# One load queue in order of need, and a batch's first projections in the tail of the batch ahead

## The chip, the cores and the metric

The kernel runs on one core of one Trainium2 chip. The metric is the device time of the kernel in microseconds; a lower number is better. The engines of a core run side by side, each through its own instructions in a fixed order: TensorE (PE) multiplies matrices into PSUM, VectorE (DVE) and ScalarE (ACT) work element by element and can read PSUM, GpSimd (POOL) does so on SBUF alone, and SyncE (SP) issues DMAs. ACT can issue DMAs too.

## The reference, cut to what matters

There are 16 batches of 512 positions, each of width 512. One block of attention and one gated FFN run on each batch:

```python
x = x + layernorm(attn(layernorm(x)))       # 16 heads of 32, causal, distance bias
x = x + layernorm(ffn(layernorm(x)))

# attn(h)
q = h @ Wq_down.T @ Wq_up.T                 # rank 384
c = h @ Wkv_down.T                          # rank 128
k, v = c @ k_up, c @ v_up                   # per head
s = q k^T / sqrt(32) - slope[h] * |i - j|   # causal
out = softmax(s) @ v  @ Wo.T

# ffn(h): weights are packed 4-bit values with a scale for each group of 128
y = (silu(h @ Wg.T) * (h @ Wu.T)) @ Wd.T    # 512 -> 2 x 1408 -> 512
y / rms(y)
```

## The kernel before, in words

**Stages of a batch.** A batch is four tiles of 128 positions. `normed(b, t)` normalises one loaded tile `xl` (statistics on VectorE, the reciprocal root on GpSimd, the scaling on VectorE), transposes it on PE and lets ScalarE copy it into `xnT`. `attention_steps(b)` then makes c (`pc`), the first k and q (`pk`, `pq`), and works through 16 units: four groups of four heads, and in each group four blocks of 128 queries, so that the scores of a unit are 128, 256, 384 or 512 wide. A unit's `scores` are four matmuls, four VectorE reductions that add the distance bias and take the row maximum (L338), four exps on ScalarE (L351), a reciprocal, and four scalings on GpSimd (L357). Two units later `turn` transposes the weights (`pt`) and copies them to `pT` (three by ScalarE, one by VectorE); three units later `attend` multiplies them with v (`po`). The first four units each make one block of v too (`pv`), and the third and fourth unit of a group make the next group's q and k. `tail(t)` multiplies by Wo (`pw`, L429), normalises, adds the input, normalises again; the result is transposed (`ptf`) and split into three bf16 parts, `x2`.

**The FFN.** `ffn_steps(b)` has 11 blocks `i`. Each block makes four gate steps (`pg`) and four up steps (`pu`) of three bf16 matmuls, each evacuated by ScalarE or VectorE in turn; then four output tiles (`py`) take 11 down steps each, which need no evacuation until the tile is done. That makes 132 steps. A finished `py` tile is normalised into `z` through two reciprocal roots on GpSimd.

**What sets the order.** PE's order is written out by hand: `interleave(main, side, share)` runs the attention of batch b as the main line, and each `yield n` in it lets n FFN steps of batch b - 1 follow. Batch 0 has no FFN ahead of it; 22 steps that unpack the FFN weights (`unpack_steps`, with a load `dq` or `dqd`, two VectorE passes, and a third on ScalarE or VectorE) run beside it at a share of 0.16. After the last attention, the last FFN runs alone. On the other engines and on SyncE's queue a scheduler sets the order when the kernel is built.

**Buffers.** `ps_m` is a PSUM pool of three slots for `pc`, `pk`, `pq`, `pv`, `pw`, `pg`, `pu`, `py` and the join of the q weights (`pjq`); `ps_s` has four for scores and transposes. `xl` has two buffers. ACT's queue issues the weight loads, SyncE's all others.

The main line's yields, in its order:

```python
project c; yield 1; project k(0); yield 1; project q(0); yield 1
for n in units (+3):
    scores(n); yield 1
    if n < 4: project_v(n)
    yield 1
    q or k of the next group; yield 1
    if n >= 12: normed(b + 1, n - 12); yield 1
    attend(n - 3); yield 1
    turn(n - 2); yield 2
for t in range(5): tail(t); yield 4; transpose and split(t - 1); yield 4
```

Of the kernel before, what the change touches and what calls it, by code (L numbers as in the profile page):

```python
# [9 lines left out]
F32 = mybir.dt.float32  # L10
F16 = mybir.dt.float16
# [3 lines left out]
ALU = mybir.AluOpType  # L15
PSUM = bass.MemoryType.PSUM

P = 128
HEADS = 16
HD = 32  # L20
# [11 lines left out]
def attn_ffn_kernel(  # L32
# [46 lines left out]

    def load_w(src, rows, cols, name, pool=const, tag=None):  # L80
        w = pool.tile([P, rows // P, cols], F32, tag=tag or name, name=name)
        nc.scalar.dma_start(w, src.rearrange("(c p) n -> p c n", p=P))
        return w

    xl_tiles = {}

    def load_norm(b):
        for t in range(NT):  # L90
            xl = work.tile([P, D], F32, tag="xl", name=f"xl_{b}_{t}", bufs=2)
            nc.sync.dma_start(xl, x_in[b, t * P : (t + 1) * P, :])
            xl_tiles[b, t] = xl

    load_norm(0)
    w_kv = load_w(wkv_t, D, RKV, "w_kv")

    w_qd = load_w(wqd, RQ, D, "w_qd", work, "v")
    w_qu = load_w(wqu_t, RQ, D, "w_qu", work, "atT")
    w_vup = load_w(vup, RKV, D, "w_vup")  # L100
    w_kup = load_w(kup, RKV, D, "w_kup")
    w_o = load_w(wo_t, D, D, "w_o")
    w_q = const.tile([P, ND, D], F32, tag="w_q", name="w_q")


    w_gu = tc.dram_tile([NI, P, NGU * P], BF16, name="w_gu")
# [6 lines left out]
    nc.gpsimd.memset(mhalf, -0.5)  # L113

    dist = const.tile([P, L], F32, tag="dist", name="dist")
    nc.gpsimd.iota(
        dist, pattern=[[1, L]], base=P - L, channel_multiplier=-1,  # L120
        allow_small_or_imprecise_dtypes=True,
    )
    nc.gpsimd.affine_select(
        out=dist, in_=dist, pattern=[[-1, L]], compare_op=ALU.is_ge,
        fill=MASKED, base=L - P, channel_multiplier=1,
    )

    qscale = const.tile([P, NG], F32, tag="qscale", name="qscale")  # L130
    for g in range(NG):
        for j in range(HPG):
            nc.gpsimd.memset(
                qscale[j * HD : (j + 1) * HD, g : g + 1], SCALE / SLOPES[g * HPG + j]
            )


    shl = const.tile([P, 1], I32, tag="shl", name="shl")
    shl0 = const.tile([P, 1], I32, tag="shl0", name="shl0")
    nc.gpsimd.iota(shl0, pattern=[[0, 1]], base=0, channel_multiplier=1)  # L140
    nc.vector.tensor_scalar(shl, shl0, 7, 7, ALU.bitwise_and, ALU.bitwise_xor)
    nc.vector.tensor_scalar(shl, shl, 2, None, ALU.logical_shift_left)

    raw = work.tile([P, NI * NGU], F16, tag="raw", name="raw")
    nc.scalar.dma_start(raw, gus)
    s_gu = const.tile([P, NI * NGU], F32, tag="s_gu", name="s_gu")
    nc.gpsimd.tensor_scalar(s_gu, raw, 1.0, None, ALU.mult)
    ups = s_gu.rearrange("p (i c) -> p i c", c=NGU)[:, :, ND:]  # L150
    nc.gpsimd.tensor_scalar(ups, ups, 0.5, None, ALU.mult)

# [97 lines left out]
            pt[:, :D].rearrange("p (c n) -> p c n", n=P),  # L252
        )

    def attention_steps(b):
        xn_t = xn_ts.pop(b)

        def project(dst, lhs, rhs, n, copy, name):
            pm = ps_m.tile([P, 512], F32, tag="pm", name=name)
            for c in range(n):  # L260
                nc.tensor.matmul(pm, lhs(c), rhs(c), start=c == 0, stop=c == n - 1)  # L261
            copy(dst, pm)  # L262

        q_ts = {}

        def project_q(g):
            q_ts[g] = work.tile([P, L], F32, tag="qT", name=f"qT_{b}_{g}", bufs=2)
            project(
                q_ts[g],
                lambda c: w_q[:, c, g * P : (g + 1) * P],  # L270
                lambda c: xn_t[:, c, :],
                ND,
                lambda o, i: nc.vector.tensor_scalar(
                    o, i, qscale[:, g : g + 1], None, ALU.mult
                ),
                f"pq_{b}_{g}",
            )

        k_ts = {}

        def project_k(g):
            k_ts[g] = work.tile([P, L], F32, tag="kT", name=f"kT_{b}_{g}", bufs=2)
            project(
                k_ts[g],
                lambda c: w_kup[:, 0, g * P : (g + 1) * P],
                lambda c: c_t,
                1,
                nc.scalar.copy,
                f"pk_{b}_{g}",
            )  # L290

        c_t = work.tile([P, L], F32, tag="cT", name=f"cT_{b}")
        project(
            c_t, lambda c: w_kv[:, c, :], lambda c: xn_t[:, c, :], ND, nc.scalar.copy,
            f"pc_{b}",
        )
        yield 1
        project_k(0)
        yield 1
        if b == 0:  # L300
            join_q()
        project_q(0)
        yield 1
        v = work.tile([P, NT, D], F32, tag="v", name=f"v_{b}")

        def project_v(t):
            project(
                v[:, t, :],
                lambda c: c_t[:, t * P : (t + 1) * P],
                lambda c: w_vup[:, 0, :],  # L310
                1,
                nc.scalar.copy if t % 2 == 0 else nc.vector.tensor_copy,
                f"pv_{b}_{t}",
            )

        at_t = work.tile([P, NG, L], F32, tag="atT", name=f"atT_{b}")

        def scores(g, qb):
            w = (qb + 1) * P
            mx = small.tile([P, HPG], F32, tag="mx", name=f"mx_{b}_{g}_{qb}")  # L320
            sums = small.tile([P, HPG], F32, tag="sums", name=f"sums_{b}_{g}_{qb}")
            ps, s = [], []
            for j in range(HPG):
                rows = slice(j * HD, (j + 1) * HD)
                st = ps_s.tile([P, 512], F32, tag="s", name=f"s_{b}_{g}_{qb}_{j}")
                nc.tensor.matmul(  # L326
                    st[:, :w],
                    q_ts[g][rows, qb * P : (qb + 1) * P],
                    k_ts[g][rows, :w],
                    start=True,  # L330
                    stop=True,
                )
                s.append(st)
            for j in range(HPG):
                p = work.tile(
                    [P, w], F32, tag=f"p{qb}", name=f"p_{b}_{g}_{qb}_{j}", bufs=HPG
                )
                nc.vector.tensor_tensor_reduce(  # L338
                    p,
                    s[j][:, :w],  # L340
                    dist[:, L - w :],
                    SLOPES[g * HPG + j],
                    -3.4e38,
                    ALU.add,
                    ALU.max,
                    mx[:, j : j + 1],
                )
                ps.append(p)
            nc.vector.tensor_scalar(mx, mx, -1.0, None, ALU.mult)  # L349
            for j in range(HPG):  # L350
                nc.scalar.activation(  # L351
                    ps[j], ps[j], AF.Exp, bias=mx[:, j : j + 1],
                    accum_out=sums[:, j : j + 1],
                )
            nc.vector.reciprocal(sums, sums)  # L355
            for j in range(HPG):
                nc.gpsimd.tensor_scalar(  # L357
                    ps[j], ps[j], sums[:, j : j + 1], 1.0, ALU.mult, ALU.mult
                )
            return ps  # L360
# [36 lines left out]
        for n in range(len(units) + lag2):  # L397
            if n < len(units):
                g, qb = units[n]
                made[n] = scores(g, qb)  # L400
                yield 1
                if n < NT:
                    project_v(n)
                yield 1
                if g + 1 < NG and qb == 2:
                    project_q(g + 1)
                elif g + 1 < NG and qb == 3:
                    project_k(g + 1)
                yield 1
                if b + 1 < B and n >= len(units) - NT:  # L410

                    normed(b + 1, n - (len(units) - NT))
                    yield 1
                if n == len(units) - NT:
                    load_x(b)
            if 0 <= n - lag2 < len(units):
                attend(*units[n - lag2], turned.pop(n - lag2))
                yield 1
            if 0 <= n - lag < len(units):
                turned[n - lag] = turn(*units[n - lag], made.pop(n - lag))  # L420
                yield 2
# [19 lines left out]
            return y  # L441

        ys = {}
        for t in range(NT + 1):
            if t < NT:
                ys[t] = tail(t)
                yield 4
            if t > 0:
                y = ys.pop(t - 1)
                pt = transpose_block(  # L450
# [90 lines left out]

    for t in range(NT):
        normed(0, t)
    for b in range(B):
        if b + 1 < B:
            load_norm(b + 1)
        if b == 0:
            interleave(attention_steps(b), unpack_steps(), 0.16)
        else:
            interleave(attention_steps(b), ffn_steps(b - 1))  # L550
# [52 lines left out]
```

## Time and profile before

| what | us |
|---|---|
| median of 3 runs | 3367.75 (3363.11 to 3371.17) |
| the profiled execution | 3367.57, span 3365.8 |
| PE busy | 3027.8 (90% of the span) |
| VectorE busy | 1894.0 (56%) |
| GpSimd busy | 1712.2 (51%) |
| ScalarE busy | 1557.2 (46%) |
| first scores of batch 0 on PE | at 51.79 |
| first Wo matmul of batch 0 | at 174.09 |
| first c matmul of batch 1 | at 209.01 |
| first gate matmul of the last FFN | at 3251.87 |

The span runs from the first to the last instruction of one profiled execution; the time of that execution stands beside it. In a line of a timeline the columns are the start, the length, the engine, the source line, the operation with the tile written and the tiles read, the shapes, and how many instructions were merged; the bracket is the engine's idle time just before, and what ended it.

### The profile page before, as it was taken

What the parts mean: (1) busy time and instruction counts of PE and PEld (TensorE: products, weight loads), DVE (VectorE), ACT (ScalarE), POOL (GpSimd) and SP (SyncE); (2) the same over time, 40 slices, a digit from 0 to 9 for tenths busy, and PEclk for the clock granted to TensorE, in tenths of its full rate; (3) what the DMA queues carried; (4) which work ended last, traced back from release to release, by engine and by line L of the source; (5) the groups of instructions that cost most, each with busy time, mean ns of one, the idle gap of its engine ahead of it and who ended that gap; (6) DMA issues with size and microseconds to landing.
All of it is one profiled execution on the core that took longest, in us unless ns stands there. A gap on an engine that the chain in (4) does not pass through costs nothing.

```text
span 3365.8 us, 49620 instructions
## 1 busy us (share of the span) xinstructions
PE 3027.8 (90%) x17304; PEld 1500.1 (45%) x17304; DVE 1894.0 (56%) x4937; ACT 1557.2 (46%) x4016; POOL 1712.2 (51%) x2412
## 2 busy tenths in 40 slices
PE   5879999989998899999999999899989999999998
PEld 2434444444444444444444444444444444444443
DVE  3556465564655556465564655646465564655643
ACT  3536264462635526264362634626255362644622
POOL 2245454554545546454554545545455554545554
PEclk9889999999999999999999999999999999999999
DMA  5201001111010100101011010101101010001000
GB/s 158 85 26 32 30 28 32 32 32 32 23 35 29 33 32 26 35 26 35 29 32 32 23 35 29 35 29 29 35 23 38 26 33 29 29 26 32 23 26 25
DMA packets 61866, 116.07 MB, mean 34 GB/s; under 512 B 6832, under 2 KB 8752, under 8 KB 61616
## 3 DMA queue, kind: packets, MB, share of 16 engines
q1 hardware_dynamic: 59328, 109.47, 10.6%
q10 hardware_dynamic: 2288, 3.43, 0.3%
q8 instruction: 137, 2.24, 0.3%
q14 instruction: 113, 0.93, 0.1%
HBM read 93.21 MB, written 19.66 MB: 34 GB/s over the span
## 4 chain that ended last, share of the span: by engine, by line
PE 46%; DVE 21%; POOL 15%; ACT 11%; issue 4%; DMA 2%; POOLq 0%; SPq 0%; ACTq 0%; DVEq 0%
PE py L507 10%; DVE p L338 8%; PE pg L481 7%; ACT p L351 7%; PE pq L261 7%; PE pu L481 6%; PE pt L371 5%; PE pw L429 4%; PE po L384 3%; PE s L326 3%; POOL p L357 3%; POOL g L497 3%; POOL hT L503 2%; POOL u L497 1%; ACT u L491 1%
## 5 line engine op out<-in xcount | busy, mean ns | idle before, releaser
L357 POOL TENSOR_SCALAR p<-p,sums 128x128 f32<-128x128 f32 (+3 forms) x1024 | 550.5, 556 | 426.2 <-DVE sums L355 291.3
L351 ACT ACTIVATE p<-p,mx 128x128 f32<-128x128 f32 (+3 forms) x1024 | 561.6, 550 | 416.5 <-DVE mx L349 416.4
L481 PEld LDWEIGHTS <-wi 128*128 128x128 bf16 x4224 | 385.6, 98 | 756.3 <-issue 452.9
L507 PE MATMUL py<-w_dn,hT 128*128 128x512 f32 x1408 | 656.1, 598 | 0.0
L481 PE MATMUL pg<-x,wi 128*128 128x512 bf16 x2112 | 541.3, 380 | 117.4 <-ACT kT L262 32.7
L481 PE MATMUL pu<-x,wi 128*128 128x512 bf16 x2112 | 533.9, 382 | 67.7 <-DVE g L493 49.4
L338 DVE CUSTOM_DVE_ANT_0 p<-s,dist 128x128 f32<-128x128 f32 (+3 forms) x1024 | 443.7, 485 | 51.2 <-PE s L326 49.1
L497 POOL TENSOR_TENSOR u<-u,u 128x512 f32<-128x512 f32 x176 | 229.0, 1301 | 349.7 <-DVE u L493 347.6
L371 PE MATMUL pt<-ident,p 128*128 128x128 f32 x2560 | 339.3, 278 | 34.2 <-ACT xnT L250 27.9
L507 PEld LDWEIGHTS py<-w_dn,hT 128*128 128x128 f32 x1408 | 252.1, 190 | 261.6 <-issue 255.6
L497 POOL TENSOR_TENSOR g<-g,g 128x512 f32<-128x512 f32 x176 | 223.4, 1269 | 273.3 <-DVE g L493 273.3
L373 ACT COPY pT<-pt 128x128 f32<-128x128 f32 (+3 forms) x768 | 273.7, 427 | 175.0 <-PE pt L371 116.4
L371 PEld LDWEIGHTS pt<-ident,p 128*128 128x128 f32 x2560 | 301.1, 143 | 111.0 <-POOL p L357 38.3
L491 ACT ACTIVATE g<-pg,s_gu 128x512 f32<-128x512 f32 x352 | 242.2, 688 | 224.3 <-PE pg L481 223.3
L493 DVE SCALAR_TENSOR_TENSOR u<-pu,s_gu,u 128x512 f32<-128x512 f32 x352 | 263.3, 748 | 114.0 <-ACT u L491 105.8
L493 DVE SCALAR_TENSOR_TENSOR g<-pg,s_gu,g 128x512 f32<-128x512 f32 x352 | 263.5, 749 | 82.8 <-ACT g L491 52.6
L491 ACT ACTIVATE u<-pu,s_gu 128x512 f32<-128x512 f32 x352 | 239.4, 680 | 76.1 <-PE pu L481 76.1
L326 PE MATMUL s<-kT,qT 32*128 32x128 f32 (+3 forms) x2048 | 246.5, 489 | 24.4 <-DVE pT L373 7.6
L355 DVE RECIPROCAL sums<-sums 128x4 f32<-128x4 f32 x256 | 45.5, 178 | 388.6 <-ACT p L351 388.6
L261 PE MATMUL pq<-xnT,w_q 128*128 128x512 f32 x512 | 243.5, 620 | 17.1 <-DVE g L493 17.1
L231 ACT CAST x<-ptf 128x512 bf16<-128x512 f32 x64 | 37.3, 583 | 473.2 <-PE ptf L225 473.2
L429 PE MATMUL pw<-w_o,atT 128*128 128x512 f32 x512 | 232.0, 596 | 0.0
(82 smaller groups left out, 3305.7 us busy)
## 6 DMA issues: line engine op xcount, KB each, us to landing
wi<-w_gu SPq DMA_DIRECT2D x176, 256.0 KB, 2.6
xl<-x_in SPq DMA_DIRECT2D x64, 256.0 KB, 2.6
x<-x_in SPq DMA_DIRECT2D x64, 256.0 KB, 2.6
out<-x SPq DMA_DIRECT2D x64, 256.0 KB, 2.0
dq<-gup SPq DMA_DIRECT2D x11, 512.0 KB, 4.8
w_gu<-wq SPq DMA_DIRECT2D x11, 256.0 KB, 2.0
dqd<-dnp SPq DMA_DIRECT2D x11, 256.0 KB, 3.8
sc<-dns SPq DMA_DIRECT2D x11, 128.0 KB, 3.4
```

Of the source, the lines that this page charges most:

```text
L261: nc.tensor.matmul(pm, lhs(c), rhs(c), start=c == 0, stop=c == n - 1)
L326: nc.tensor.matmul(st[:, :w], q_ts[g][rows, qb * P : (qb + 1) * P], k_ts[g][rows, :w], start=True, stop=True,)
L338: nc.vector.tensor_tensor_reduce(p, s[j][:, :w], dist[:, L - w :], SLOPES[g * HPG + j], -3.4e38, ALU.add, ALU.max, mx[:, j : j + 1],)
L351: nc.scalar.activation(ps[j], ps[j], AF.Exp, bias=mx[:, j : j + 1], accum_out=sums[:, j : j + 1],)
L357: nc.gpsimd.tensor_scalar(ps[j], ps[j], sums[:, j : j + 1], 1.0, ALU.mult, ALU.mult)
L371: nc.tensor.transpose(pt[:, cols], ps[j][:, cols], ident)
L429: nc.tensor.matmul(pm[:, :D], at_t[:, g, t * P : (t + 1) * P], w_o[:, g, :], start=g == 0, stop=g == NG - 1,)
L481: nc.tensor.matmul(pm[:, :L], wi[:, o, :], x2_p[b][:, n, c, :], start=n == 0, stop=n == 2,)
L491: nc.scalar.activation(to, pm[:, :L], AF.Copy, scale=s)
L493: nc.vector.scalar_tensor_tensor(to, pm[:, :L], s, to, ALU.mult, ALU.add)
L497: nc.gpsimd.tensor_tensor(acc, acc, add, ALU.add)
L507: nc.tensor.matmul(pm[:, :D], h_t[:, i, t * P : (t + 1) * P], w_dn[:, i, :], start=i == 0, stop=i == NI - 1,)
```

## The change

It has four edits.

1. All first loads are issued by SyncE, in this order: the four `xl` tiles of batch 0, w_kv, w_kup, w_vup, w_qd, w_qu; the scales `raw` and w_o follow later. The `xl` tiles have four buffers. The constants `dist`, `qscale` and the scales `s_gu` are made after the first layernorms in program order.
2. c, k(0), q(0) and all four blocks of v of a batch are made by `Projections.first()`. For batch 0 it runs ahead of the main line. For batch b + 1 it is stepped once after each `tail(t)` of batch b.
3. The yields around v go: the first three of the main line, and one of each unit. The tail has one more yield for each of its four tiles. The main line had 135 steps and has 120.
4. `load_norm` is called for one tile at a time.

```diff
-        nc.scalar.dma_start(w, src.rearrange("(c p) n -> p c n", p=P))
+        nc.sync.dma_start(w, src.rearrange("(c p) n -> p c n", p=P))
...
-            xl = work.tile([P, D], F32, tag="xl", name=f"xl_{b}_{t}", bufs=2)
+        xl = work.tile([P, D], F32, tag="xl", name=f"xl_{b}_{t}", bufs=NT)
...
+    for t in range(NT):
+        load_norm(0, t)
     w_kv = load_w(wkv_t, D, RKV, "w_kv")
+    w_kup = load_w(kup, RKV, D, "w_kup")
+    w_vup = load_w(vup, RKV, D, "w_vup")
     w_qd = load_w(wqd, RQ, D, "w_qd", work, "v")
     w_qu = load_w(wqu_t, RQ, D, "w_qu", work, "atT")
-    w_vup = load_w(vup, RKV, D, "w_vup")
-    w_kup = load_w(kup, RKV, D, "w_kup")
-    w_o = load_w(wo_t, D, D, "w_o")
...
+        def first(self):
+            self.make_c()
+            yield
+            self.make_k(0)
+            if self.b == 0:
+                join_q()
+            self.make_q(0)
+            yield
+            for t in range(NT):
+                self.make_v(t)
+                if t % 2:
+                    yield
...
                 made[n] = scores(g, qb)
                 yield 1
-                if n < NT:
-                    project_v(n)
-                yield 1
                 if g + 1 < NG and qb == 2:
-                    project_q(g + 1)
+                    p.make_q(g + 1)
                 elif g + 1 < NG and qb == 3:
-                    project_k(g + 1)
+                    p.make_k(g + 1)
                 yield 1
...
         ys = {}
+        ahead = iter(())
+        if b + 1 < B:
+            pr[b + 1] = Projections(b + 1)
+            ahead = pr[b + 1].first()
         for t in range(NT + 1):
             if t < NT:
                 ys[t] = tail(t)
                 yield 4
+                next(ahead, 0)
+                yield 1
...
+    raw = work.tile([P, NI * NGU], F16, tag="raw", name="raw")
+    nc.sync.dma_start(raw, gus)
...
+    nc.sync.dma_start(w_o, wo_t.rearrange("(c p) n -> p c n", p=P))
+
+    pr[0] = Projections(0)
+    for _ in pr[0].first():
+        pass
     for b in range(B):
-        if b + 1 < B:
-            load_norm(b + 1)
+        for t in range(NT):
+            if b + 1 < B:
+                load_norm(b + 1, t)
```

More of the change, by code (lines that the diff above doesn't have):

```diff
@@ L81, in load_w, with load_norm @@
         w = pool.tile([P, rows // P, cols], F32, tag=tag or name, name=name)
-        nc.scalar.dma_start(w, src.rearrange("(c p) n -> p c n", p=P))
+        nc.sync.dma_start(w, src.rearrange("(c p) n -> p c n", p=P))
         return w
     xl_tiles = {}
-    def load_norm(b):
-        for t in range(NT):
-            xl = work.tile([P, D], F32, tag="xl", name=f"xl_{b}_{t}", bufs=2)
-            nc.sync.dma_start(xl, x_in[b, t * P : (t + 1) * P, :])
-            xl_tiles[b, t] = xl
-    load_norm(0)
+    def load_norm(b, t):
+        xl = work.tile([P, D], F32, tag="xl", name=f"xl_{b}_{t}", bufs=NT)
+        nc.sync.dma_start(xl, x_in[b, t * P : (t + 1) * P, :])
+        xl_tiles[b, t] = xl
+    for t in range(NT):
+        load_norm(0, t)
     w_kv = load_w(wkv_t, D, RKV, "w_kv")
+    w_kup = load_w(kup, RKV, D, "w_kup")
+    w_vup = load_w(vup, RKV, D, "w_vup")
     w_qd = load_w(wqd, RQ, D, "w_qd", work, "v")
     w_qu = load_w(wqu_t, RQ, D, "w_qu", work, "atT")
-    w_vup = load_w(vup, RKV, D, "w_vup")
-    w_kup = load_w(kup, RKV, D, "w_kup")
-    w_o = load_w(wo_t, D, D, "w_o")
     w_q = const.tile([P, ND, D], F32, tag="w_q", name="w_q")
+    w_o = const.tile([P, ND, D], F32, tag="w_o", name="w_o")
     w_gu = tc.dram_tile([NI, P, NGU * P], BF16, name="w_gu")
@@ L113, in attn_ffn_kernel @@
     nc.gpsimd.memset(mhalf, -0.5)
[L118 to L135, printed above, removed]
     shl = const.tile([P, 1], I32, tag="shl", name="shl")
@@ L142, in attn_ffn_kernel @@
     nc.vector.tensor_scalar(shl, shl, 2, None, ALU.logical_shift_left)
[L146 to L151, printed above, removed]
     def join_q():
@@ L253, in normed, with __init__, project @@
         )
-    def attention_steps(b):
-        xn_t = xn_ts.pop(b)
-        def project(dst, lhs, rhs, n, copy, name):
+    class Projections:
+        def __init__(self, b):
+            self.b = b
+            self.q, self.k = {}, {}
+        def project(self, dst, lhs, rhs, n, copy, name):
             pm = ps_m.tile([P, 512], F32, tag="pm", name=name)
@@ L262, in project, with make_c, make_q @@
             copy(dst, pm)
[L264 to L269, printed above, removed]
+        def make_c(self):
+            b, xn_t = self.b, xn_ts[self.b]
+            self.c = work.tile([P, L], F32, tag="cT", name=f"cT_{b}")
+            self.project(
+                self.c, lambda c: w_kv[:, c, :], lambda c: xn_t[:, c, :], ND,
+                nc.scalar.copy, f"pc_{b}",
+            )
+        def make_q(self, g):
+            b, xn_t = self.b, xn_ts[self.b]
+            self.q[g] = work.tile([P, L], F32, tag="qT", name=f"qT_{b}_{g}", bufs=2)
+            self.project(
+                self.q[g],
                 lambda c: w_q[:, c, g * P : (g + 1) * P],
@@ L277, in project_q, with make_k @@
             )
[L279 to L284, printed above, removed]
+        def make_k(self, g):
+            b = self.b
+            self.k[g] = work.tile([P, L], F32, tag="kT", name=f"kT_{b}_{g}", bufs=2)
+            self.project(
+                self.k[g],
                 lambda c: w_kup[:, 0, g * P : (g + 1) * P],
-                lambda c: c_t,
+                lambda c: self.c,
                 1,
@@ L290, in project_k, with make_v @@
             )
[L292 to L296, printed above, removed]
-        yield 1
[L298 to L309, printed above, removed]
+        def make_v(self, t):
+            b = self.b
+            if t == 0:
+                self.v = work.tile([P, NT, D], F32, tag="v", name=f"v_{b}")
+            self.project(
+                self.v[:, t, :],
+                lambda c: self.c[:, t * P : (t + 1) * P],
                 lambda c: w_vup[:, 0, :],
@@ L314, in project_v, with attention_steps @@
             )
+        def first(self):
[10 more added lines that the diff above has]
+                    yield
+    pr = {}
+    def attention_steps(b):
+        p = pr.pop(b)
+        q_ts, k_ts, v = p.q, p.k, p.v
         at_t = work.tile([P, NG, L], F32, tag="atT", name=f"atT_{b}")
@@ L334, in scores @@
             for j in range(HPG):
-                p = work.tile(
+                pj = work.tile(
                     [P, w], F32, tag=f"p{qb}", name=f"p_{b}_{g}_{qb}_{j}", bufs=HPG
@@ L338, in scores @@
                 nc.vector.tensor_tensor_reduce(
-                    p,
+                    pj,
                     s[j][:, :w],
@@ L347, in scores @@
                 )
-                ps.append(p)
+                ps.append(pj)
             nc.vector.tensor_scalar(mx, mx, -1.0, None, ALU.mult)
@@ L401, in attention_steps @@
                 yield 1
-                if n < NT:
-                    project_v(n)
-                yield 1
                 if g + 1 < NG and qb == 2:
-                    project_q(g + 1)
+                    p.make_q(g + 1)
                 elif g + 1 < NG and qb == 3:
-                    project_k(g + 1)
+                    p.make_k(g + 1)
                 yield 1
@@ L543, in attn_ffn_kernel @@
         normed(0, t)
+    dist = const.tile([P, L], F32, tag="dist", name="dist")
+    nc.gpsimd.iota(
+        dist, pattern=[[1, L]], base=P - L, channel_multiplier=-1,
+        allow_small_or_imprecise_dtypes=True,
+    )
+    nc.gpsimd.affine_select(
+        out=dist, in_=dist, pattern=[[-1, L]], compare_op=ALU.is_ge,
+        fill=MASKED, base=L - P, channel_multiplier=1,
+    )
+    qscale = const.tile([P, NG], F32, tag="qscale", name="qscale")
+    for g in range(NG):
+        for j in range(HPG):
+            nc.gpsimd.memset(
+                qscale[j * HD : (j + 1) * HD, g : g + 1], SCALE / SLOPES[g * HPG + j]
+            )
+    raw = work.tile([P, NI * NGU], F16, tag="raw", name="raw")
+    nc.sync.dma_start(raw, gus)
+    s_gu = const.tile([P, NI * NGU], F32, tag="s_gu", name="s_gu")
+    nc.gpsimd.tensor_scalar(s_gu, raw, 1.0, None, ALU.mult)
+    ups = s_gu.rearrange("p (i c) -> p i c", c=NGU)[:, :, ND:]
+    nc.gpsimd.tensor_scalar(ups, ups, 0.5, None, ALU.mult)
+    nc.sync.dma_start(w_o, wo_t.rearrange("(c p) n -> p c n", p=P))
+    pr[0] = Projections(0)
+    for _ in pr[0].first():
+        pass
     for b in range(B):
-        if b + 1 < B:
-            load_norm(b + 1)
+        for t in range(NT):
+            if b + 1 < B:
+                load_norm(b + 1, t)
         if b == 0:
```

## The prediction, on record before the changed kernel ran

> **What bounds the kernel now.** I read the page first, then TensorE's waits, then its timeline at the start, in batch 0 and over one whole later batch, and last the VectorE and GpSimd timelines beside TensorE's longest waits. The page says that TensorE (PE) is the engine to watch:
>
> ```profile
> PE 3027.8 (90%) x17304; PEld 1500.1 (45%) x17304; DVE 1894.0 (56%) x4937; ACT 1557.2 (46%) x4016; POOL 1712.2 (51%) x2412
> PE   5879999989998899999999999899989999999998
> PEclk9889999999999999999999999999999999999999
> ```
>
> PE is loose in the first two slices only. After that a batch is worth what its PE work and its PE waits are worth. The start, from PE's timeline:
>
> ```profile
> 25.78 1.12 PE L225 MATMUL pta<-ident,xl 128*128 128x128 f32 x4 [16.20 <-DVE xl L220]
> 29.21 6.18 PE L261 MATMUL pc<-xnT,w_kv 128*128 128x512 f32 x8 [0.67 <-ACT xnT L250]
> 51.79 0.50 PE L326 MATMUL s<-kT,qT 32*128 32x128 f32 x8 [0.85 <-DVE qT L273]
> ```
>
> The third x tile was loaded only at 16.41 us, because `xl` had two buffers and SyncE had queued eight later `x` loads ahead of it; PE waited 16.20 us for it. The first softmax instruction stands at 55.25 us on VectorE.
>
> The stretches (us; busy PE, PEld, DVE, ACT, POOL; then granted clock, DMA share, GB/s) are two of batch 0 and two of batch 2, its tail last:
>
> ```profile
> 51.00:110.00 59.00, 46.49 (x264) 26.21 (x265) 32.01 (x113) 33.26 (x101) 18.05 (x32) 0.79 0.28 81
> 174.00:209.00 35.00, 19.61 (x50) 9.38 (x49) 23.89 (x44) 3.61 (x6) 16.33 (x26) 0.80 0.11 34
> 448.00:516.00 68.00, 64.15 (x476) 33.95 (x475) 45.45 (x122) 45.25 (x121) 40.50 (x51) 1.00 0.08 24
> 569.00:614.00 45.00, 43.62 (x144) 20.38 (x144) 20.81 (x43) 4.09 (x7) 21.21 (x34) 1.00 0.11 36
> ```
>
> Batch 0's tail has 15 us of idle PE; the later tails have almost none, though the other engines are half idle there. The waits of a later batch repeat to a hundredth of a microsecond. PE's timeline over 1221 to 1427 us:
>
> ```profile
> 1221.99 0.63 PE L225 MATMUL ptf<-ident,y 128*128 128x128 f32 x4 [1.38 <-DVE y L220]
> 1230.97 0.81 PE L481 MATMUL pg<-x,wi 128*128 128x512 bf16 x3 [2.26 <-DVE z L527]
> 1231.62 5.29 PE L261 MATMUL pq<-xnT,w_q 128*128 128x512 f32 x8
> 1249.68 3.70 PE L261 MATMUL pq<-xnT,w_q 128*128 128x512 f32 x8 [1.15 <-DVE g L493]
> 1298.21 1.45 PE L481 MATMUL pg<-x,wi 128*128 128x512 bf16 x6 [1.09 <-ACT kT L262]
> 1344.99 2.72 PE L481 MATMUL pu<-x,wi 128*128 128x512 bf16 x6 [2.24 <-DVE g L493]
> 1362.70 0.30 PE L371 MATMUL pt<-ident,p 128*128 128x128 f32 x1 [1.80 <-ACT xnT L250]
> ```
>
> The brackets are idle PE time and its releaser. With the smaller ones they sum to 16.6 us of the 204.5 us from 1223.32 to 1427.85: 1.4 in the tail, 5.7 at the start (through the fourth unit), 4.1 in the middle groups, 5.4 late. The late 2.24 is VectorE standing still for GpSimd's rstd of the next batch's layernorm:
>
> ```profile
> 1343.73 0.55 DVE L220 TENSOR_SCALAR xl<-xl,mva,ra 128x512 f32<-128x512 f32 x1 [2.76 <-POOL ra L214]
> ```
>
> The period differs from batch to batch (201.7 to 204.5 us) because of the 5.29 above: eight pq matmuls take 3.44 us in other batches, and 1.7 more in 7 of 14, just after the 2.26 us wait.
>
> **The change, part by part.** PE prices from the rows: an FFN step (three bf16 matmuls) 0.65 us, a down step 0.86, c or q 3.44, k or one v block 0.86.
>
> *First loads.* The four `xl` loads now lead one queue, c's and the other weights follow, and ScalarE issues none, so its table load no longer waits until 17.31 us. Two tiles were in use at 3.79 and 5.24; four in one queue at about 0.7 us for each 256 KB (some 380 GB/s in the trace) land by about 5.5, and w_qu, last of 3.25 MB, by 12 to 14, before it is needed. Four statistics and rstds (0.9 us of VectorE each) and transposes end near 11.5, so c starts at 11.6 instead of 29.2. c (6.2, cold), its copy, k, the 10.5 us weight join, q and four v blocks (3.4, formerly after the first scores) reach the first softmax near 39.3: **-16 us**. The unpack chain is the catch. One dq step (load 4.8, two VectorE passes 1.45, ScalarE 1.06, write issue) has a period of 8 to 10, and its first load now stands behind 5 MB, so the chain starts later, not earlier. VectorE meets three dq steps before its first softmax instead of five, 13 instead of 14 by the first Wo result (-2), and two more in the tail, 1.6 us each less two layernorms moved out (+2).
>
> The Trainium skill, page "DMA: Bandwidth & Descriptors", section "Issuing engines are not separate DMA queues", says that all queues share the same 16 DMA engines, so one queue changes order and issue time, not bandwidth; by it alone the loads would be worth no more than the order.
>
> *Projections into the tail.* PE work is the same in each later batch, but batch 1's c, k, q, v (3.44 + 0.86 + 3.44 + 3.44 = 11.2 us) fall into batch 0's 15 idle us: **-11**. What covered the end of the x2 split is gone there: the last ACT, DVE, ACT, POOL steps (0.6, 0.7, 0.6, 1.2) are met by one 0.44 us scores group: **+3**. Batch 0 sums to -16 - 2 + 2 - 11 + 3 = **-24** (bounds: -11 if the unpack chain eats most of it, -35 if it never binds).
>
> *The later tails.* A batch's main steps fall from 135 to 120 against 132 FFN steps, so the last gate/up steps follow the first Wo matmul, and 12 down steps are left for after the tail; those are dense PE work and cost nothing. PE's matmuls rotate through three PSUM slots. The first Wo result holds one through statistics, rstd and normalising (about 2.9 us by the DVE rows), and u's accumulations queue behind it on VectorE: c starts 1.3 us late. A down result holds another for 6.7 us (z, in the rows), so the second v block of each pair waits for the first's copy: about 1.0 us, twice. The 1.4 us ptf wait goes, as more PE work precedes it. 3.3 - 1.4 = **+1.9** a batch (bounds -1.4, +4).
>
> *The batch start.* With four `xl` buffers, the loads come early, and the order on VectorE puts all four layernorms (5.2 us) between the first three units' softmax, beside z of the last down tile. I laid the changed order of each engine out by hand with the rows' durations, from the last down matmul on. PE's fourth FFN step waits 1.5 (statistics, rstd and z ahead of g on VectorE); the third scores 1.0; the eighth FFN step 2.6 (q's scaling stands behind three layernorm parts); in the fourth unit VectorE waits 2.3 for an rstd that GpSimd queues behind an add and hT, which delays transposes 1.7, and the kT copy and the pT copies that follow cost 2.1 and 0.7. Sum 10; laid out the same way, z of the kernel before comes out a tenth long, so I take 9.0 where 5.7 stood: **+3.3** (bounds 0 and +6).
>
> *Middle and late.* A unit now holds five FFN steps for six. The chain through the widest unit (four reductions, four exps, kT copy) lasted 8.1 us from its scores and stays, so **+0.4**. Late, the 2.24 and 0.89 go with their layernorms, and the xnT copy (1.80) costs 0.8 more with less PE work ahead of it: 2.9 for 5.4, **-2.5** (bounds -4, 0).
>
> *Clock.* The start's waits resemble the one that lowered the clock in half the batches (1.7 us each). I let it happen in all: 7 x 1.7 = **+12**.
>
> A rule against the change: the Trainium skill, "TensorE: Matmul & The Clock Gate", Part 1, says that the array falls to half speed after an idle window of about 3.4 us; by it, waits under 3.4 us are free of this and the +12 would be 0. In the rows a wait of 2.26 was already enough in 7 of 14, so I go by the rows.
>
> **Sum.** -24 + 15 x (3.3 + 0.4) + 14 x (1.9 - 2.5) - 2 (the last batch's 2.35 us ptf wait goes) + 12 = **+33**. The profiled execution took 3367.57 us (span 3365.8), 0.2 from the median 3367.75; so 3400, taken as **3399**.
>
> **Rivals.** (a) *The crowd at the start is hidden*: PE waits there no more than the old 5.7. It decides if VectorE's g and q evacuations come no later than the third following FFN step. Then neither 49 (15 x 3.3) nor 12 is paid: 3399 - 61 = 3338, faster. For it: VectorE is only 56% busy; against: in-order waits are what the rows show, not load. Chance 0.22. (b) *The unpack chain takes the early start back*: dq loads bound batch 0, the 16 us are lost, 3415. For it: the first half of the chain in the profile runs through dq loads. 0.15. (c) *The clock stays low through the starts*, as at 51 to 110 us (0.79 with PE 79% busy): 18 us of PE work in each of 15 starts at 0.8 adds 4.5, in all 67 less the 12: 3454. 0.10. My forecast, 3370 to 3430: 0.53.
>
> **Numbers.** A difference of 0.2% (7 us) is what a measurement here can tell. Faster 0.25: (a) and a little of the forecast's edge. Same 0.07. Slower 0.68. The range 3335 to 3440 holds (a), the forecast and (b), and leaves out (c) and the edges. One side holds most of it.
>
> **What would show it.** Right: first scores on PE near 37 us; batch 1's scores near 190; in later batches new waits at pv, pc and, for the first four units, at pg, pu and pt on DVE; no 2.2 us wait late. Wrong: start waits under 6 us a batch, late waits as before, or a first softmax after 45 us.

## The result, and the profile after

The changed kernel takes **3460.65 us** (median of 4 runs, 3459.92 to 3464.5) beside 3367.01 for the kernel before on the same chip: a ratio of 1.028 (95% interval 1.0262 to 1.0298), 93.6 us slower. The forecast was 3399, range 3335 to 3440. The profiled execution took 3464.5 us, its span 3462.7. From the profile's page, after:

```profile
PE 3129.2 (90%) x17058; PEld 1558.6 (45%) x17304; DVE 1864.9 (54%) x4937; ACT 1564.3 (45%) x4016; POOL 1719.4 (50%) x2412
```

PE is busy for 101 us more (3027.8 before) though no matmul was added (17304 weight loads in both; 246 matmul records are missing from this trace). So the same matmuls last longer. The mean granted clock of the span fell with it, from 0.984 to 0.956. The clock held back 0.044 x 3462.7 = 152 us after and 0.016 x 3365.8 = 54 before, 98 more; the span grew by 96.9. That the two numbers are nearly equal does not yet show that one makes the other.

The startup went as forecast. PE's timeline of the changed kernel:

```profile
9.28 3.67 PE L195 MATMUL pta<-ident,xl 128*128 128x128 f32 x16 [9.28 <-DVE xl L190]
...
13.63 3.70 PE L234 MATMUL pc<-xnT,w_kv 128*128 128x512 f32 x8 [0.68 <-ACT xnT L220]
...
36.23 0.50 PE L313 MATMUL s<-kT,qT 32*128 32x128 f32 x8
```

The first scores stand at 36.23 (51.79 before, "near 37" forecast), batch 0's first Wo matmul at 153.70 for 174.09, and batch 1's first scores at 197.05 for 220.69: 24 us won. From there on the kernel loses. One later batch of each kernel, first Wo matmul to first Wo matmul; the columns are us, busy time (and instructions) of PE, PEld, DVE, ACT and POOL, then granted clock, DMA share and GB/s. Before:

```profile
1181.40:1385.90 204.50, 187.78 (x1081) 92.70 (x1080) 116.15 (x305) 96.31 (x250) 106.66 (x149) 0.98 0.10 30
```

After, the batch and then the stretches of the next batch's attention:

```profile
1183.10:1395.20 212.10, 193.06 (x1066) 95.48 (x1081) 114.22 (x306) 96.80 (x250) 107.26 (x149) 0.96 0.10 29
...
1253.00:1267.00 14.00, 12.18 (x57) 5.72 (x58) 11.15 (x44) 9.03 (x32) 9.40 (x18) 1.00 0.17 54
1267.00:1288.00 21.00, 15.88 (x86) 7.29 (x88) 12.49 (x37) 10.05 (x28) 10.82 (x17) 0.84 0.04 14
1288.00:1309.00 21.00, 20.90 (x161) 10.40 (x161) 13.74 (x38) 12.88 (x33) 12.98 (x18) 1.00 0.09 26
1309.00:1323.00 14.00, 11.46 (x70) 5.80 (x68) 7.15 (x23) 8.93 (x26) 6.42 (x7) 0.76 0.05 19
1323.00:1372.00 49.00, 45.83 (x360) 25.41 (x365) 31.25 (x90) 34.09 (x91) 28.62 (x40) 1.00 0.14 39
1372.00:1388.00 16.00, 12.13 (x82) 6.16 (x81) 8.09 (x19) 9.19 (x21) 8.10 (x9) 0.89 0.13 34
1388.00:1465.00 77.00, 74.59 (x261) 34.71 (x261) 30.38 (x58) 12.62 (x22) 30.91 (x44) 1.00 0.07 25
```

The clock is full except in three short stretches, and there this batch's 0.96 is made. PE's timeline shows what stands in them:

```profile
1269.24 1.44 PE L471 MATMUL pu<-x,wi 128*128 128x512 bf16 x3 [2.43 <-DVE qT L253]
...
1280.79 0.81 PE L471 MATMUL pu<-x,wi 128*128 128x512 bf16 x3 [1.96 <-ACT kT L235]
...
1282.60 2.59 PE L471 MATMUL pu<-x,wi 128*128 128x512 bf16 x6
...
1313.94 0.59 PE L471 MATMUL pg<-x,wi 128*128 128x512 bf16 x1 [1.96 <-ACT kT L235]
...
1316.05 2.74 PE L471 MATMUL pg<-x,wi 128*128 128x512 bf16 x6
...
1381.74 0.63 PE L358 MATMUL pt<-ident,p 128*128 128x128 f32 x2 [2.14 <-ACT xnT L220]
```

Beside each of these waits of about 2 us stand matmuls at half speed: six FFN matmuls in 2.59 and 2.74 us where they take 1.46 elsewhere in the same batch. Such a spell of half clock lasts 3.41 us and holds back 1.7 us; the one at 1313.94 is twice as long. This batch has five of them (8.53 us), the batch of the kernel before two (3.42); that kernel has nine in 13 batches.

To compare kernels I use four numbers of a later batch, each a mean over the 13 batches between the second batch's and the fifteenth's first Wo matmul: the period, the idle time in the timeline's brackets (**waits**), the sum of one minus the granted clock over windows of 1 us (**clock**), and what is left (**rest**: PE's work and the small gaps inside a row).

| kernel | time | period | waits | clock | rest |
|---|---|---|---|---|---|
| before | 3367 to 3374 | 203.3 | 17.3 | 1.2 | 184.8 |
| after | 3460.7 | 211.7 | 17.5 | 8.5 | 185.6 |
| before + load edit | 3269.3 | 197.3 | 12.7 | 0.0 | 184.6 |
| the same, five steps a unit | 3379.2 | 204.8 | 16.8 | 1.7 | 186.3 |
| after, six steps a unit | 3314.9 | 201.4 | 12.5 | 3.0 | 185.9 |
| after, v in the units | 3369.9 | 204.8 | 15.3 | 2.2 | 187.3 |
| after, kT by VectorE | 3427.9 | 208.4 | 17.0 | 2.6 | 188.8 |
| after, shifted by one step | 3452.2 | 210.7 | 19.5 | 4.5 | 186.8 |
| after + useless matmuls | 3624.2 | 221.8 | 11.6 | 7.9 | 202.3 |

After against before, the waits are the same in sum; 7.3 of the 8.4 us a batch stand under the clock. That is an account, not yet a cause, and it adds up two edits that turned out to be of opposite sign.

### The profile page after: what moved, and what is told of

Same layout as the page of the kernel before. It is cut to its first block, busy times and chain, and to the rows that moved or that the text cites. A ratio compares the mean times of both kernels' runs of the same rounds, so it can differ in the third digit from the quotient of the medians.

```text
span 3462.7 us, 49545 instructions
## 1 busy us (share of the span) xinstructions
PE 3129.2 (90%) x17058; PEld 1558.6 (45%) x17304; DVE 1864.9 (54%) x4937; ACT 1564.3 (45%) x4016; POOL 1719.4 (50%) x2412
## 3 DMA queue, kind: packets, MB, share of 16 engines
q8 instruction: 138, 2.26, 0.3%
## 4 chain that ended last, share of the span: by engine, by line
PE 64%; DVE 12%; ACT 9%; POOL 9%; issue 4%; DMA 2%; SPq 0%; POOLq 0%; DVEq 0%; ACTq 0%
PE py L497 17%; PE pu L471 10%; PE pg L471 8%; ACT p L338 6%; PE pt L358 6%; DVE p L325 6%; PE pq L234 5%; PE s L313 5%; PE pw L413 4%; PE po L371 4%; POOL p L344 2%; POOL g L487 2%; PE pv L234 2%; PE pc L234 1%; DVE g L483 1%
## 5 line engine op out<-in xcount | busy, mean ns | idle before, releaser
L344 POOL TENSOR_SCALAR p<-p,sums 128x128 f32<-128x128 f32 (+3 forms) x1024 | 561.2, 566 | 405.7 <-DVE sums L342 296.0
L471 PE MATMUL pu<-x,wi 128*128 128x512 bf16 x2003 | 580.8, 404 | 101.2 <-ACT kT L235 48.3
L471 PE MATMUL pg<-x,wi 128*128 128x512 bf16 x1975 | 555.8, 395 | 84.5 <-ACT kT L235 29.4
L497 PE MATMUL py<-w_dn,hT 128*128 128x512 f32 x1408 | 630.9, 593 | 0.0
L497 PEld LDWEIGHTS py<-w_dn,hT 128*128 128x128 f32 x1408 | 263.3, 190 | 306.9 <-issue 306.3
L313 PE MATMUL s<-kT,qT 32*128 32x128 f32 (+3 forms) x2048 | 308.8, 521 | 21.4 <-DVE mx L325 11.6
L487 POOL TENSOR_TENSOR g<-g,g 128x512 f32<-128x512 f32 x176 | 223.4, 1270 | 186.3 <-DVE g L483 160.8
L234 PE MATMUL pq<-xnT,w_q 128*128 128x512 f32 x512 | 236.4, 606 | 0.0
L493 POOL TENSOR_TENSOR hT<-th,u 128x512 f32<-128x512 f32 x176 | 223.8, 1272 | 9.3
L313 PEld LDWEIGHTS s<-kT,qT 32*128 32x128 f32 x2048 | 149.8, 201 | 159.8 <-issue 65.6
```

Source lines behind the costliest of these rows:

```text
L313: nc.tensor.matmul(st[:, :w], q_ts[g][rows, qb * P : (qb + 1) * P], k_ts[g][rows, :w], start=True, stop=True,)
L344: nc.gpsimd.tensor_scalar(ps[j], ps[j], sums[:, j : j + 1], 1.0, ALU.mult, ALU.mult)
L471: nc.tensor.matmul(pm[:, :L], wi[:, o, :], x2_p[b][:, n, c, :], start=n == 0, stop=n == 2,)
L487: nc.gpsimd.tensor_tensor(acc, acc, add, ALU.add)
L497: nc.tensor.matmul(pm[:, :D], h_t[:, i, t * P : (t + 1) * P], w_dn[:, i, :], start=i == 0, stop=i == NI - 1,)
```

## The experiments

**The two edits apart.** First the whole load edit without the projections: one queue, four `xl` buffers, tables built later.

> The kernel before with the whole load edit (one queue, four xl buffers, tables built later) and nothing of the projections: six FFN steps a unit, v in the first four units. Theory A (clock: the changed kernel loses 0.044 of 3462.7 us = 152 us of TensorE clock against 0.016 of 3365.8 = 54, because five FFN steps a unit leave waits of about 2 us after which the clock drops): the start's 15.6 us are won and little is lost, 3345, granted clock 0.98 or more. Theory B (the four early layernorms that four xl buffers allow crowd VectorE at each batch start, and their waits drop the clock): most of the loss appears here, 3410 to 3440, clock near 0.96. Theory C (the projections in the tail, through three PSUM slots): 3345.

Measured: 3269.31 us, ratio 0.9698 (0.9684 to 0.9712), 102 us **faster** than before. Theories A and C gave the sign but not the size; B is out. Its timeline in a later batch (one batch in the first line, as a window):

```profile
1136.10:1333.30 197.20, 183.55 (x1067) 91.47 (x1080) 116.38 (x305) 96.28 (x250) 106.67 (x149) 1.00 0.11 32
```

```profile
1185.69 3.70 PE L231 MATMUL pq<-xnT,w_q 128*128 128x512 f32 x8 [1.61 <-DVE z L497]
...
1310.10 0.30 PE L341 MATMUL pt<-ident,p 128*128 128x128 f32 x1 [0.72 <-ACT xnT L220]
```

The wait for z is 1.61 for 2.26, the late 2.24 for VectorE's g is gone, the late 1.80 is 0.72. No wait of that batch reaches 2 us, and the clock never drops in the 13 batches.

Then the projections alone, with the loads and two `xl` buffers as they were:

> The kernel before with the projections alone moved into the tail (five FFN steps a unit), its loads and two xl buffers as they were. Theory A: 3430 to 3475, granted clock near 0.96. Theory B (early layernorms): 3355 to 3375. Theory C (tail slots): each tail costs several us, 3430 to 3475, but with the clock low in the tails and not in the units.

3476.76 us, ratio 1.0315 (1.0299 to 1.033), 106 us slower, and the low clock stands in the units. So the loads are worth -102, the projections +106 alone and +191 on top of the loads (3460.65 - 3269.31).

**Which part of the load edit.** The kernel before with this line alone changed:

```diff
-            xl = work.tile([P, D], F32, tag="xl", name=f"xl_{b}_{t}", bufs=2)
+            xl = work.tile([P, D], F32, tag="xl", name=f"xl_{b}_{t}", bufs=NT)
```

> The kernel before with one edit: four xl buffers for two; its queues, its order of loads and its tables stay. The load edit as a whole gave 3269.3. Theory A1 (a batch is 6 us shorter there because the layernorms of the next batch's tiles come out of the late units, with the 2.24 and 1.80 us waits and the slow spells of the clock that follow waits of 2 us): the batches gain all of it here too and only batch 0's start, up to 16 us, is missing: 3270 to 3290, granted clock 0.985 or more. Rival A2 (the one queue and its order make the batches shorter, or less work for another engine): 3340 to 3370, with 203 us a batch.

3276.54, ratio 0.9722 (0.9708 to 0.9737): 94 of the 102 us. The queue and the order are worth the other 7, all in batch 0, whose first Wo matmul comes at 164.31 here and at 157.16 with the whole edit. The same line undone in the changed kernel:

> The changed kernel with two xl buffers for four, so that two of the next batch's layernorms cannot run before the late units; nothing else. Theory A: only the start's 2.43 us wait with its slow spell may go (15 x about 2.5 us), and batch 0 starts about 10 us later: 3430 to 3470. Theory B (early layernorms): most of the loss goes, 3365 to 3395. Theory C: 3460 to 3475.

3476.27, 16 us more than the changed kernel. Its later batches are as long as the changed kernel's (a period of 211.6 us in both); 10 of the 16 us are batch 0's later start (first Wo matmul at 164.12 for 153.70). So two buffers for four cost 94 us in the kernel before and nothing in the changed kernel's later batches. That waits and spells of another origin already fill them is my reading; no run shows it.

**Which part of the projections' edit.** The edit also takes out one `yield 1` in each unit, the one behind `project_v`. Put back:

```diff
                 made[n] = scores(g, qb)
                 yield 1
+                yield 1
                 if g + 1 < NG and qb == 2:
                     p.make_q(g + 1)
```

> The changed kernel with one empty step put back into each unit, so that a unit again holds six FFN steps for its five; nothing else. Theory A (clock, by way of the sparser units): the waits for the kT copy fall from 1.96 to about 1.1, the clock returns to 0.98, some 85 of the 93 us come back: 3360 (3335 to 3385). Theory B (early layernorms at the start): a little comes back, 3430 to 3455. Theory C (tail slots): 3440 to 3465.

3314.88, ratio 0.9834 (0.9819 to 0.9849): the empty step is worth **146 us**, and the changed kernel with it is faster than the kernel before. A batch has 5.0 us less waiting and 5.5 less of the clock. The move itself, with the step put back, still costs 46 us beside the loads alone (3314.88 for 3269.31). The kT waits of 1.96 us are gone; what stands in their place in a group:

```profile
1260.38 0.81 PE L472 MATMUL pu<-x,wi 128*128 128x512 bf16 x3 [0.96 <-DVE g L484]
```

The reverse, the load edit alone with one of the units' empty steps taken out:

> The kernel with the load edit alone (3269.3) and one empty step less in each unit, so five FFN steps a unit as in the changed kernel; the projections stay where the kernel before has them. Density theory (five steps for six leave TensorE too little work over the chain of reductions and exps, whatever stands in the tail): most of the 146 us that the step was worth in the changed kernel, 3350 to 3410, clock 0.975 or less. Rival (it costs only together with the projections in the tail): 3265 to 3300.

3379.16, ratio 1.0035 (1.0022 to 1.0048), 110 us more than with six; waits 16.8 for 12.7 a batch. So the missing step costs without the projections in the tail too.

**v.** The changed kernel with the four `pv` blocks back in the first four units, still at five steps:

> The changed kernel with the v blocks in the first four units, as before; c, k and q in the tail, five FFN steps a unit. Theory A: the first group's waits (1.26, 2.43, 1.96) are covered by four times 0.86 us, with up to two spells, and the two 0.67 waits of the tail go; the other groups' kT waits and spells stay: 15 x 5 = 75 less, 3370 to 3420. Theory C (the tail's PSUM slots alone): 1.4 a batch, 3435 to 3445.

3369.87, ratio 1.0001 (0.9992 to 1.0011): 91 us come back. In the batch that I read, the first group's waits, its kT copy included, are 5.2 us for 6.8, none is over 1.5, and no spell stands beside them; that the 0.86 us of a v block does there what an FFN step would is my reading. The 91 here and the 146 above are more together than the 191 that the projections cost on top of the loads, so they are not two shares of it. The wait for kT in the second group is still there, and starts a spell still; the third group's (1.35) started none in the batch that I read:

```profile
1282.95 0.38 PE L469 MATMUL pg<-x,wi 128*128 128x512 bf16 x1 [1.96 <-ACT kT L235]
```

**The kT copy.** In the changed kernel VectorE copies kT, so that it need not stand behind four exps:

```diff
                 lambda c: self.c,
                 1,
-                nc.scalar.copy,
+                nc.vector.tensor_copy,
                 f"pk_{b}_{g}",
```

> The changed kernel with the kT copy on VectorE for ScalarE, where it need not stand behind four exps; five FFN steps a unit as in the changed kernel. Theory A (slow spells of the clock, 3.4 us at half speed and 1.7 us each, are started by waits of about 2 us, most of them for the kT copy): the three kT waits of 1.3 to 2.0 a batch go, with three of the five spells: 15 x (5.2 + 5.1) = 155 at most, 100 to 155 in all: 3305 to 3360. Rival (ScalarE's evacuation of the next FFN step stands behind the same four exps and takes the wait's place): 3440 to 3465, same clock.

3427.91, ratio 1.0169 (1.0154 to 1.0184): 33 us for the 100 to 155 expected. The waits did not shrink but changed their releaser:

```profile
1261.79 0.81 PE L471 MATMUL pu<-x,wi 128*128 128x512 bf16 x3 [2.44 <-DVE qT L253]
...
1270.02 0.81 PE L471 MATMUL pg<-x,wi 128*128 128x512 bf16 x3 [0.29 <-DVE kT L235]
...
1273.22 1.02 PE L313 MATMUL s<-kT,qT 32*128 32x128 f32 x6 [1.32 <-ACT pT L360]
```

kT's 1.96 is 0.29, and the next scores wait 1.32 for a pT copy on the same ScalarE. The clock's part fell by 5.9 us a batch and the period by 3.3, as the rest rose by 3.1: in this run the spells taken away gave back about half of what the account puts down to them. The same edit in the kernel with the loads alone:

> The kernel with the load edit alone, and the kT copy on VectorE for ScalarE. If the wait for kT (2.16 us a batch) is worth its length: 3235 to 3250. Rival (another copy behind ScalarE's exps takes its place, as the pT copy did in the changed kernel): 3265 to 3300.

3280.7, ratio 0.9723 (0.9707 to 0.9739), 11 us more than without it: as the rival said, FFN steps that ScalarE evacuates wait instead.

**q at the batch start.** The kernel with six steps waits at the start of a batch for the x2 split, since no projection covers it there:

```profile
1403.92 0.48 PE L313 MATMUL s<-kT,qT 32*128 32x128 f32 x2 [1.11 <-DVE xr L202]
...
1406.40 0.59 PE L472 MATMUL pg<-x,wi 128*128 128x512 bf16 x1 [1.45 <-POOL x L204]
```

So q was put back there, first with an empty step behind it, then without:

```diff
         q_ts, k_ts, v = p.q, p.k, p.v
+        p.make_q(0)
+        yield 1                              # left out in the second version
```

> The kernel with six steps a unit (3314.9) and q's first projection back at the batch start, so that its 3.44 us of TensorE work cover the end of the x2 split; c, k and v stay in the tail. Theory: the waits at the start for the split (1.11 for xr and 1.46 for x) and the two slow spells that follow them go: 14 x (2.6 + 1.7 to 3.4) = 60 to 84, less what z's place on VectorE costs, as in the kernel with the loads alone (1.5 for z ahead of q): 3250 to 3285. Rival (q's scaling on VectorE now makes the scores wait as long as the split did): 3300 to 3320.

> q's first projection at the batch start as in the kernel of 3417.4, without the empty step behind it, so that the FFN steps stand against the units as in the kernel of 3314.9. Phase theory: 3265 to 3310, since q covers the end of the x2 split. Rival (q's place is the cause: the first scores wait 2.7 for its scaling): 3380 to 3425.

3417.44, ratio 1.0139 (1.0122 to 1.0155), and 3337.54, ratio 0.991 (0.9895 to 0.9924). Both lose to 3314.9. Without the extra step, the split is covered but the first scores stand still for q's scaling on VectorE, longer than for the split:

```profile
1215.16 0.81 PE L313 MATMUL s<-kT,qT 32*128 32x128 f32 x8 [3.95 <-DVE qT L253]
```

With it 80 us more are lost, so the place of the FFN steps against the units was tried by itself: one empty step at the start of each batch's attention, with the projections in the tail and six steps, then five; two such steps with six; and one with the loads alone.

```diff
+        yield 1
         units = [(g, qb) for g in range(NG) for qb in range(NT)]
```

> The kernel with six steps a unit (3314.9) and one empty step at the start of each batch's attention; q stays in the tail. Phase theory (the 102 us that moving q to the start cost came from the one step that was added with it): 3380 to 3430, with waits of 18 us a batch for 12. Rival (q's place was the cause): 3300 to 3325.

> The changed kernel with one empty step at the start of each batch's attention: five FFN steps a unit as before, but each of them one place earlier against the units. Density theory: the time hardly changes, 3445 to 3475. Phase theory (what counts is which engine, ScalarE or VectorE, evacuates the step that stands ahead of a kT copy or a row of exps): waits change by over 2 us a batch, below 3430 or above 3490.

> The kernel with six steps a unit and the projections in the tail (3314.9) and two empty steps at the start of each batch's attention, where one gave 3421.2. Phase theory (ScalarE's and VectorE's steps are back in their places): 3300 to 3340. Rival (FFN steps ahead of the first scores wait for the split, two as well as one): 3400 to 3440.

> The kernel with the load edit alone and one empty step at the start of each batch's attention. Phase theory: as with six steps and the projections in the tail (106 us for the same step), 3340 to 3390. Rival (the shift costs only where an FFN step then waits for the end of the x2 split, which c and q cover here): 3260 to 3290.

Six steps shifted by one: 3421.18 (ratio 1.0158, 1.0141 to 1.0174), 106 us for one empty step a batch. Shifted by two: 3420.58, so the phase theory, by which two steps restore the order, falls. Five steps shifted: 3452.2, 8 less, though the clock's part of a batch is nearly halved (4.5 us for 8.5): the waits rose by 2.0 and the rest by 1.1. The loads alone, shifted: 3325.1, 56 more, between the two expectations. An FFN step ahead of the first scores then needs the split early, as this batch of the kernel with six steps and one shift shows:

```profile
1236.34 0.38 PE L473 MATMUL pg<-x,wi 128*128 128x512 bf16 x1 [0.67 <-ACT x L201]
1237.92 0.38 PE L473 MATMUL pg<-x,wi 128*128 128x512 bf16 x1 [1.20 <-ACT x L203]
1240.15 0.58 PE L473 MATMUL pg<-x,wi 128*128 128x512 bf16 x1 [1.86 <-POOL x L204]
```

These 3.7 us stand for 2.6 without the shift, a small part of the 6.8 us that a batch is longer. Most of what is left stands in the units: two waits of 1.1 us a group (VectorE's u, then kT) for one of 0.96.

**More steps, and useless ones.** Seven FFN steps a unit, in the kernel with the loads alone:

> The kernel with the load edit alone (3269.3, 12.8 us of TensorE waits a batch), with one empty step more in each unit: seven FFN steps for six. Density theory: the two waits of 1 us a group (0.96 for a VectorE evacuation, 1.09 for the kT copy) go, 15 x 3 to 5: 3190 to 3230. Phase theory (an odd number breaks the order of ScalarE's and VectorE's steps against the units as five did): 3330 to 3400.

3618.77, ratio 1.072 (1.0704 to 1.0736), which neither theory expected. Its PE waits name the cause (us in total, times, longest us):

```profile
PE ptf L195 <- DVE mva L179: 100.8, 13, 7.8
PE pta L195 <- DVE xl L190: 96.3, 15, 9.2
PE ptf L195 <- DVE y L190: 76.7, 19, 11.0
```

The FFN is used up too early: in the batch from 1252.66 (its first Wo matmul) the down steps began at 1201.65 and the last of them stands at 1273.70, ahead of the fourth Wo block. What the two layernorms of the later tiles (`ptf`) and the next batch's layernorm (`pta`) take then stands uncovered. The FFN's steps are a stock: five a unit leave too few in the units, seven too few in the tail.

Last, five useless matmuls ahead of each attend step, in the changed kernel and, as the control, with the loads alone:

```diff
+            for _ in range(5):
+                nc.tensor.matmul(
+                    po[g][:, qb * P : (qb + 1) * P], ident, ident, start=True, stop=True
+                )
             for kb in range(qb + 1):
```

> The changed kernel with five useless matmuls (128x128, float32, identity times identity) ahead of each attend step, written to the part of po that the next matmul starts anew: 16 x 0.7 = 11.2 us of TensorE work a batch, 179 us in all, that no other engine sees. Clock theory: up to half of it falls into the waits and most of the five slow spells (9 us a batch) go: 3400 to 3510. Rival (order of the FFN steps; the clock only follows the time): all of it is paid, 3600 to 3640.

> The kernel with the load edit alone (3269.3, no slow spell in a later batch) and the same useless matmuls: the control. Clock theory: only waits can hide them, at most 4 of 11.2 us a batch: 3375 to 3450, so 105 to 180 more. Rival: 179 more as in the changed kernel, 3430 to 3450.

3624.2 (ratio 1.0755, 1.0737 to 1.0773) and 3467.27 (1.0288, 1.0273 to 1.0303): 164 and 198 us more. Five of them add 0.97 us of busy PE (3376.8 - 3129.2 over 256), not 0.7. In the changed kernel they took 5.8 us of waits a batch away, but hardly any of the clock's part (7.9 for 8.5):

```profile
1242.80:1464.60 221.80, 209.47 (x1224) 116.00 (x1241) 114.08 (x306) 97.37 (x250) 107.42 (x149) 0.96 0.09 28
```

My clock theory expected most spells to go; it is wrong in this. A busier PE is not enough; the four longest waits left in that batch (1.27 for g, 1.96 and 1.45 for kT, 2.55 for pT) still had a spell beside each of them.

**Best version.** The load edit alone, 3269.3 us, beats both kernels, by 3% and by 5.5%; nothing added to it here made it faster.

## Why the prediction was wrong

**Start of the kernel (-24): held.** First scores at 36.23, batch 1's first scores 23.6 us earlier. That c would run cold was wrong (3.70 us, not 6.2).

**Batch start (+3.3): wrong sign for the load edit.** I let the four early layernorms crowd VectorE and charged each batch 9.0 us of waits for 5.7. In the changed kernel the batch from 1253.23 has 6.8, with two long waits (2.43 for qT where 2.6 was forecast, 1.96 for kT where 2.1 was). With the loads alone the start's waits are 5.6, no more than before. Rival (a), the hidden crowd, was right about the loads; the longest wait there is 1.61 for 2.26, and no spell stands beside it.

**Late (-2.5): the gain was there, and hidden.** The 2.24 went, as forecast. With the loads alone the late waits are 1.6 for 5.4, 3.8 us gained. In the changed kernel I forecast 2.9 and found 5.6: xnT's copy keeps PE waiting 2.14, less than the 2.6 forecast, but four waits of 0.5 to 0.9 us that I had not foreseen stand beside it (xnT again, u twice, mx).

**Middle (+0.4): the step that failed.** I saw that a unit holds five FFN steps for six and called the steps left for the tail "dense PE work" that costs nothing. They cost little there; they are missed in the units, beside a chain of reductions, exps and copies. That step is worth 146 us with the projections in the tail and 110 without, for the 6 us (15 x 0.4) in my sum. I priced it by the sum of the waits, and that sum did not move: in the batch shown the waits changed by +0.6 in the tail, +1.1 at the start, -0.2 in the middle and +0.2 late, and over 13 batches they are as long as before, where I forecast 3.1 more. What changed is their length: a kT wait is 1.96 where it was 1.09, while others went. Few long waits replaced many short ones, and the time stands under the clock, the next term.

**Clock (+12): the right kind of loss, eight times too small.** I let spells follow the start's wait alone, one a batch. They stand beside the waits for kT and xnT too, five in the batch shown: by the account above 98 us in the span, though no run shows that all of it would come back without them. The Trainium skill's rule in the prediction ("TensorE: Matmul & The Clock Gate", Part 1: half speed after an idle window of 3.4 us) would have made it 0; waits of 1.96 us with spells beside them refute that use of it. The same page's section "A second HAM failure mode: psum-queue depth-cycling" fits better: it says that short idle gaps between groups of matmuls, from cycling through PSUM buffers, let the clock swing between half and full. The kT waits above are such: pu waits for the PSUM slot that kT's copy has yet to empty. Rival (c) named the clock, but put it in the starts.

**Tail (+1.9): too much, inside its bounds.** The 0.67 us waits at pv and the one of 0.62 for y come to 2.0 a batch where I had 3.3, so +0.6 with the 1.4 that went.

**What stays open.** What else, beside PE's idle time in a step of the clock's grid (last section), decides on a spell. Why just six steps in just this place are good: density would explain five against six and a drained stock explains seven, but a shift by one step costs 56 to 106 us with six and nothing with five, and by two it costs as much as by one. And how much of the clock's 98 us would come back if only the clock were mended: taking spells away through kT's copy gave back half, and the shift with five steps (4.1 us a batch less under the clock, 0.9 less in the period) under a quarter.

## What to carry to other kernels

When an edit takes an empty step out of a hand-made interleave, price it as work moved away from every wait that it covered, not as work moved; count the stock of covering work through all stages. Read the granted clock in windows of a few us beside the longest PE waits: here, in the changed kernel's batch, a spell that held back 1.7 us stood beside each wait of about 2 us, and two kernels with the same sum of waits (17.3 and 17.5 us a batch) differed by 8.4 us in the period. Measure the parts of a combined edit apart: here one line of buffers was worth 94 us, and the rest of the edit buried it.

## What the hardware showed that I had not expected

Slow spells come in one size, 3.41 us with 1.7 us held back, or in multiples of it. Waits of 1.96 to 2.43 us in the batch of the changed kernel each had one; with kT on VectorE a wait of 2.44 had none, and with five steps and the loads alone neither had this one:

```profile
1281.65 1.45 PE L296 MATMUL s<-kT,qT 32*128 32x512 f32 x8 [2.04 <-ACT pT L343]
```

Waits of 1.6 us and less, alone, had none in the kernel with the loads alone. With useless matmuls around them, waits of 1.27 and 1.45 did, so the length of the wait is not the whole condition.

The traces hold most of the answer. In each of them the granted clock changes only on the marks of one grid of 3.413 us that runs through the whole trace (to within 0.006 us). The spells of the changed kernel's batch (the double one taken as one) begin at 1269.14, 1282.79, 1313.51 and 1381.78, which are 4, 9 and 20 such steps apart. A step at half clock follows a step in which PE was idle for long, and a wait that a mark cuts in two counts in two steps. The wait of 2.43 in the changed kernel (first two lines), then the one of 2.44 with kT on VectorE, in windows that are steps of the grid; the third number from the end is the granted clock:

```profile
1265.72:1269.14 3.41, 1.08 (x7) 0.55 (x6) 1.88 (x6) 1.70 (x6) 2.30 (x7) 1.00 0.00 0
1269.14:1272.55 3.41, 3.31 (x11) 0.77 (x10) 2.20 (x6) 0.00 (x0) 2.94 (x5) 0.50 0.15 50
...
1257.45:1260.86 3.41, 1.90 (x11) 1.05 (x10) 1.83 (x6) 2.54 (x10) 2.40 (x7) 1.00 0.00 0
1260.86:1264.28 3.41, 2.48 (x14) 0.94 (x14) 3.41 (x9) 0.00 (x0) 3.31 (x6) 1.00 0.07 20
```

PE is idle for 2.33 us of the first step, and half clock follows; the second wait is cut into 1.51 and 0.93, and the clock stays full. Over 250 to 3150 us of all 20 traces here, a half-clock step never followed a full-clock step with under 1.0 us of idle PE (14635 steps) and always followed one with over 2.1 (201 steps). Between the two it followed 269 of 1533 steps; what decides there is not shown.
